# Cross-attention on one core: three weight sums and the eight mask biases made by GpSimd, not VectorE, under a new order table

## The chip, the core and the metric

One core of a Trainium2 chip runs the whole kernel. Its engines are TensorE (PE; its weight loads are shown as PEld), VectorE (DVE), ScalarE (ACT), GpSimd (POOL) and SyncE (SP), which only issues transfers. Each has its own list of instructions and works through it in order; between engines there are semaphores. The metric is the device time of one execution in microseconds (us), lower is better.

## The reference

Eight batches of 256 queries by 1024 features attend to 256 context rows each, with 32 heads of 32 features. All of it is fp32.

```python
mu, var = mean(x), var(x)                       # over the 1024 features
q = ((x - mu) * rsqrt(var + 1e-5) * gamma + beta) @ Wq.T
scores = einsum('bhsd,bhtd->bhst', heads(q), heads(ctx)) / sqrt(32)
probs = softmax(where(mask, scores, -inf))
attn = einsum('bhst,bhtd->bhsd', probs, heads(ctx))
out = x + merge(attn) @ Wout.T
```

Keys and values are both the context itself. The mask has one bit per context row.

## The kernel before, in words

**Slots.** The work is cut into 64 slots, n = 8b + g: batch b, and a group g of four heads (128 features). A slot has, in this order: scores on TensorE (`sc`, 16 matmul records of 256 columns), a softmax on VectorE, ScalarE and GpSimd, and the product of probabilities and values two slots later (`pv`). In the softmax of a slot (`softmax_parts`, from L970) VectorE makes for each head j `e = min(sc + mb, ...)` and its minimum `mn` in one instruction per 128 queries (shown as CUSTOM_DVE_ANT_0 in the profile and as ISA in the order), ScalarE takes the exponential and the sum `den`, VectorE the reciprocal `rden`, GpSimd (for some heads ScalarE) scales `e` by `rden` in two instructions of 256 columns, and VectorE transposes `e` in 32 by 32 blocks into `pT`. `mb` is the mask bias of the batch, 0 or minus 3e38 per context row, made from the mask bytes by `mask_bias` (L919). One buffer serves all batches, so the bias of batch b can be written only when the last `e` of batch b-1 has been made. It is written during slot 8b-2, ahead of the softmax of slot 8b, which stands in the program a slot early.

**Projections.** The query projection (by Wq) of batches 2 to 7 is done for two batches at a time, and the output projection (by Wout) for the two halves of a batch, in Strassen-Winograd form: seven products in place of eight, on sums of blocks of the weights and of the activations. The weight sums T1 to T4 of both matrices are made once, in the first 200 us: `sum_wq` (L840) writes `wq` and, for T1, `ring`; `sum_wo` (L542) writes `wo`. One sum is 128 partitions by 512 elements. T1 = B12 - B11 of Wq has four parts (o = 0 to 3), and T1, T2, T3, T4 of Wout four chunks each (c = 0 to 3), where T4 = B21 - T2. TensorE's products with them are `pq_P` (queries), `po_A` and `po_S` (output). Half of the queries of batches 0 and 1 is made in the same form early on (`ph_P`). `fold` (L725) multiplies gamma into Wq. GpSimd also makes the activation sums (`xnT`, `s`, `at`), adds kept products to the residual (`r<-r,p`), and issues some loads and stores.

**What sets the order.** The kernel is first recorded as a list of calls and then issued in the order of a table of call numbers (`ORDER`, L153; `issue`, L367). So almost every instruction has the line L374 in the profile and is found by its tile names. A second table (`PLAN`, L37) says in which slot each weight sum is recorded and by which engine (`P` GpSimd, `V` VectorE).

```python
def sum_wq(to, o, engine=nc.gpsimd):
    engine.tensor_tensor(weights(to, o), weights(a, o), weights(b, o), ALU.subtract)
...
for n, which, o, *e in WQ_SUMS:
    sums[n].append(partial(sum_wq, which, o, ENGINES[e[0] if e else "P"]))
```

In the table VectorE has three of the 32 weight sums: T1 of Wq, o = 2 and 3 (`ring<-wq`), and chunk 1 of T1 of Wout (`wo<-wo`; the sums of Wout are numbered, 3 is T1).

Of the kernel before, what the change touches and what calls it, by code (L numbers as in the profile page):

```python
# [36 lines left out]
PLAN = {'wq': [[7, 'T1', 0, 'P'], [7, 'T1', 1, 'P'], [10, 'T2', 0, 'P'], [10, 'T2', 1, 'P'], [14, 'T1', 2, 'V'],  # L37
# [116 lines left out]
32-33 35 34 36-38 42 40 43 39 41 50 44 47 52 45-46 54 56 55 58 57 59-60 85 0-15 61-62 64 63 65-66 68 16 69-70  # L154
17 71 18-20 72 21-22 73-77 23-25 80-81 78 83-84 67 86-87 26 79 82 88 27-28 89 29-30 97-98 90-95 101 99 31 102
100 103-112 132 123-126 133 170 96 113 115-117 114 127-130 145-146 171 119-120 131 134 121-122 118 135-136
141-144 147-148 151-156 149-150 157-158 172-173 137 159-160 138-139 163-164 161-162 167 182 165-166 175-177
192-199 290 174 191 348 51 471 49 715 140 168 180 183 178-179 184 169 187-189 185 181 186 190 212 200-201
208-210 202-203 213 211 204 214 205 215 206-207 220-221 216-219 223 222 226-227 230 228-229 231 234 246 252
251 254-256 253 320 318 321 349 48 289 225 224 291 370 236 232-233 244 238 235 247-248 243 237 257-264 273 267  # L160
274 265 275 277 266 278-279 276 268-269 280 498 245 249-250 281-283 285-286 284 271 288 287 53 294-296 311 314
310 313 297 322 332 270 272 333 324-325 472 292-293 500 372 300 298-299 301 326 503 375 302-304 327-331
334-335 376-377 312 315 239 323 340-342 317 352 364 305 343 316 353 381 390-421 336 454 337 455 338-339 382
504-505 356 240 354 344-345 355 360 358 362 306 365 357 359 361 371 307 373 378-380 383-389 456-463 363
422-453 480 464 484 482 486 466 488 490 492 374 465 467 493 481 478 483 476 485 475 487 499 524-525 516-523
526 528 527 529-530 554 347 308 346 241 470 555 469 468 350-351 574 546 501 532 560 506 564 580 242 583
508-509 489 507 510 513 511 533 319 536 531 534-535 512 537 540 538-539 541-542 547 491 576 548-549 558-559
477 544 550 366 561 568 562-563 551 565-567 569 502 577 575 584 515 514 479 657-658 543 585-592 659-664
593-624 673 473-474 625-656 674 683 367 665-666 578-579 689 570 687 667 669 685 693 545 691 695 668 670 684
686 681 678 688 690 677 692 710 717-732 763 700 761 701 494 733-734 694 746 735-736 744 703 756 745 747 771  # L170
775-776 709 741 772 553 552 706 672 705 309 671 770 556-557 778 773 704 869 711 676 675 897 748-749 737
750-755 680 762 495-496 368 708 766 769 767 779 902 908 865 909 696 941 853-854 942 855-860 781-788 863 891
861 764 880 893 738 702 740 739 777 707 774 369 743 742 864 862 886 889 878 882 884 892 881 890 879 883 885
765 866 905 894 937 943 938 944 939-940 789-852 929-936 945 947-949 1000 867-868 912 1572 926 581 712 714 780
716 928 679 713 768 1016 887-888 898-899 910 921-922 895-896 900-901 903 907 906 923 965-968 946 951 950
952-953 969-972 875 911 924 955 757 957-959 954 960-964 977 697-698 984 973-974 571-572 870-871 913 975-976
876 904 914 916 915 497 982-983 873 999 1005 699 573 1017-1019 1224 979 978 986 985 925 682 988-989 980-981
758-759 920 991-993 956 990 995 1015 997 996 1014 1020-1024 1089-1092 1095-1096 872 1025-1088 1105-1106
1097-1098 994 998 1001-1002 1004 1003 919 1113-1116 1109 1107-1108 1110 1118 1111 1120-1121 987 1117 1119 1102
1112 1124 1134 1007 1006 1143 760 1153-1167 1218 1216-1217 917 1145 1011 1360 1122-1123 874 918 1093 1128 1130  # L180
1132 1131 1168 1171-1172 1100 1175-1176 1125-1127 877 1094 1169 1173-1174 1103 1099 1135 1133 1170 1189
1184-1187 1136 1181 1179 1177 1191 1190 1183 1182 1192 1196 1202-1203 1129 1137 1180 1197 1178 1225-1296
1301-1304 1311 1319 1309 1317-1318 1193 1198 1320 1195 1194 1315 1313 1310 1312 1359 927 1101 1149 1199-1200
1104 1013 1204 1209 1138 1210 1215 1147 1144 1140 1208 1305-1308 1150 1333-1335 1330-1331 1201 1316 1325
1327-1328 1151 1142 1323-1324 1321-1322 1340 1188 1337-1338 1326 1339 1152 1220 1346-1347 1205-1207 1146 1141
1009 1139 1008 1214 1212-1213 1010 1148 1219 1314 1348 1362-1369 1373-1378 1297-1298 1379 1299 1380 1300 1387
1385-1386 1329 1336 1381 1342-1343 1345 1383 1388-1389 1344 1349 1390 1382 1384 1401 1391-1393 1398 1396
1405-1406 1332 1397 1399 1410 1415 1407 1414 1412 1411 1420 1437-1444 1357 1370-1372 1509-1512 1640 1361 1394
1402-1403 1395 1221 1358 1222 1404 1408 1517-1518 1350 1341 1352 1211 1351 1525 1527-1528 1416 1519 1526 1409
1538 1413 1400 1417 1419 1355 1418 1428 1531 1540 1536-1537 1529-1530 1532 1539 1567 1570 1430-1431 1541-1542  # L190
1435 1573-1580 1445-1508 1513-1516 1429 1555 1354 1581 1636 1422 1356 1421 1631 1353 1641 1544-1546 1434 1520
1533-1535 1436 1547 1549-1552 1568 1582 1601 1597-1598 1554 1524 1553 1583-1585 1595 1543 1591 1593 1556 1602
1592 1596 1522 1594 1610 1608 1603-1604 1612-1614 1606-1607 1523 1599-1600 1521 1609 1619 1637-1638 1223 1432
1616-1618 1562 1605 1715 1586 1643-1650 1587 1716-1717 1588 1718 1589-1590 1651-1714 1737-1738 1548 1557-1559
1566 1621 1623-1624 1615 1622 1569 1639 1741-1742 1729 1735 1739-1740 1424 1627 1736 1625 1730 1756 1727-1728
1628 1626 1746-1747 1750 1748-1749 1620 1743 1423 1752 1754 1425 1757 1751 1758-1759 1745 582 1744 1764
1782-1789 1719-1720 1776 1721 1777 1722-1726 1778 1790 1807 1805 1761-1763 1806 1809 1642 1803-1804 1753 1799
1765 1791-1795 1810 1733 1808 1824 1426 1801 1767 1820 1563 1816 1818 1814 1839 1560 1629-1630 1561 1760 1766
1427 1633 1611 1632 1826 1825 1802 1768-1770 1731-1732 1800 1817 1815 1832 1564 1838 1012 1772 1844-1853
1796-1797 1854 1798 1855-1857 2050 1780 1433 1821-1822 1827 1565 1571 1773 1933 1811-1813 1734 1774 1858-1920  # L200
1937 1829 1823 1831 1779 1830 1935-1936 1828 1934 1939-1940 1931 1833 1938 1932 1944 1953 1834 1947 1945 1957
1929-1930 1952 1946 1835 1837 1836 1771 1843 1755 1948 1968 1841 1840 1985-1992 1921-1928 1980-1981 2198
1954-1955 1960 1941 1842 1973 1942 1958-1959 1943 1634 2008-2009 2006-2007 1949-1950 1635 1951 1965-1966 1962
1964 1963 1781 1969 1956 1979 1982 1984 1993 2021-2022 1967 1994-1999 2019 2023 2004 2014-2015 2012 1775 1976
1819 2010 2020 2013 2005 1970 2025 2024 2032 2002-2003 1961 1972 1971 2027 2016 2030 2049 2034 2017 2033 2018
1974 2029 2028 2037 2053-2060 2044-2045 2000-2001 2125-2126 2143 2145-2146 2154 2026 2031 2156 2035 2149
2137-2138 2135 2147-2148 2036 2157-2158 2150 2038 2136 2155 2181 2163 2151 2180 2182 2199-2206 2061-2124
2127-2134 2142 2144 2141 2159 2168 2193-2194 2275 2048 2051-2052 1983 2165 2153 2164 2152 2160-2161 2047
2170-2171 2169 2046 2197 2225 2162 2166 2219 2223-2224 2172 2209-2210 2207 2211 2208 2212-2218 2174 2220 2226
2229 2231 2230 2259 2221 2227-2228 2222 2140 2232 2240-2241 2236 2234 2237 2243 2242 2235 2139 2249 2183 2250  # L210
2600 2041 1975 1978 2039 2192 2040 1977 2167 2233 2175 2267 2011 2042 2173 2189 2184 2188 2190 2187 2277-2284
2271 2350-2351 2349 2352-2354 2370-2371 2258 2246 2360-2361 2260 2404-2405 2043 2355-2357 2408 2274 2238 2276
# [126 lines left out]
ALU = mybir.AluOpType  # L339

P = 128
HEADS = 32
LN_EPS = 1e-5
MASKED = 3.0e38
# [35 lines left out]
def xattn_kernel(  # L380
# [11 lines left out]
    nc = tc.nc  # L392
# [43 lines left out]
    nc = Recorded(nc)  # L436
# [113 lines left out]
    mks = {}  # L550
# [1211 lines left out]
```

## Time and profile before

| what | us |
|---|---|
| median of three runs | 564.69 (564.21 to 567.4) |
| the profiled execution itself | 564.37 |
| its span, first to last instruction | 562.6 |
| PE busy | 553.0 |
| DVE busy | 467.3 |
| ACT busy | 436.3 |
| POOL busy | 410.2 |

The times on a page or a timeline are counted from the span's start. A timeline row has start, length, engine, line, operation, output and inputs, how many instructions are merged in it, and in brackets the idle time ahead of it with what ended that. Matmuls in fp32 show two records for one call. A row of the windows view has the busy time of each engine in one stretch and the mean clock that TensorE was granted (1.00 is full). The chain is followed back from the last instruction, at each step to what released it.

### The profile page before, as it was taken

How to read it: one execution, taken by the hardware profiler on the slowest of the kernel's cores; microseconds unless marked ns; L12 is line 12 of the kernel's file. 1: busy time of each engine (PE TensorE's matmuls, PEld its weight loads, DVE VectorE, ACT ScalarE, POOL GpSimd, SP SyncE). 2: the span in 40 equal slices, each digit the busy share in tenths (PEclk: the TensorE clock that was granted, in tenths of full speed). 3: DMA queues.
4: the chain of work that ended last, by engine and by line, in shares of the span. 5: the costliest groups of instructions: out<-in, count | busy, mean ns of one | idle time of the engine just before them, and what ended most of it. 6: DMA issues, size and time to landing. Idle time of an engine off the chain costs nothing.

```text
span 562.6 us, 18616 instructions
## 1 busy us (share of the span) xinstructions
PE 553.0 (98%) x6570; PEld 368.9 (66%) x6570; DVE 467.3 (83%) x1703; ACT 436.3 (78%) x1463; POOL 410.2 (73%) x619
## 2 busy tenths in 40 slices
PE   7999999998999999999999999999999999999997
PEld 6877877655666776667666676666776577645544
DVE  5999999788898889879788889878687888788725
ACT  3698979895896679878877779878869868979920
POOL 2689989897979937569967786477874786367663
PEclk9999999998999999999999999999999999999999
DMA  8988667688558767985767767787766638755433
GB/s 299 378 254 241 179 170 171 182 233 252 144 195 284 258 165 215 246 248 171 202 172 216 210 180 211 231 212 182 222 188 197 201 96 246 205 138 157 119 81 132
DMA packets 48325, 113.67 MB, mean 202 GB/s; under 512 B 9960, under 2 KB 11624, under 8 KB 48232
## 3 DMA queue, kind: packets, MB, share of 16 engines
q1 hardware_dynamic: 42232, 92.55, 58.0%
q0 software_dynamic: 5712, 19.93, 11.5%
q8 instruction: 52, 0.85, 0.6%
q14 instruction: 41, 0.34, 0.2%
q10 hardware_dynamic: 288, 0.01, 0.0%
HBM read 59.91 MB, written 12.70 MB: 129 GB/s over the span
## 4 chain that ended last, share of the span: by engine, by line
PE 90%; DVE 6%; DMA 2%; issue 1%; POOL 1%; ACT 1%; SPq 0%; DVEq 0%; ACTq 0%; POOLq 0%
PE pq_P L374 26%; PE po_S L374 19%; PE sc L374 11%; PE pv L374 11%; PE po_A L374 10%; PE pq L374 4%; PE ph_P L374 3%; PE po_end L374 3%; DVE pT L374 2%; DVE e L374 1%; DMA v_all<-in_kv_dram 1%; PE po_last L374 1%; DVE ring L374 1%; PE px L374 1%; DMA x<-in_x_dram 1%
## 5 line engine op out<-in xcount | busy, mean ns | idle before, releaser
L374 ACT ACTIVATE e<-e,mn 128x256 f32<-128x256 f32 x512 | 256.4, 503 | 60.2 <-DVE mn L374 53.1
L374 POOL TENSOR_SCALAR e<-e,rden 128x256 f32<-128x256 f32 x368 | 172.4, 483 | 105.4 <-DVE rden L374 89.9
L374 DVE STREAM_TRANSPOSE pT<-e 128x512 f32<-128x512 f32 x256 | 175.6, 699 | 31.5 <-POOL e L374 20.2
L374 DVE CUSTOM_DVE_ANT_0 e<-sc,mb 128x256 f32<-128x256 f32 x512 | 191.3, 410 | 6.0 <-PE sc L374 3.8
L374 PE MATMUL pq_P<-xnT,wq 128*128 128x256 f32 x544 | 133.2, 382 | 0.0
L374 PEld LDWEIGHTS pq_P<-xnT,wq 128*128 128x128 f32 x544 | 101.9, 190 | 46.9 <-issue 31.5
L374 ACT ACTIVATION_READ_ACCUMULATOR e<-e,mn 128x1 f32 x512 | 97.4, 190 | 0.0
L374 ACT COPY pc<-pT 128x512 f32<-128x512 f32 x128 | 76.7, 612 | 8.3 <-DVE pT L374 6.0
L374 PE MATMUL po_S<-wo,at 128*128 128x512 f32 x152 | 75.3, 600 | 1.9 <-POOL wo L374 1.9
L374 PE MATMUL po_A<-wo,at 128*128 128x512 f32 x128 | 61.1, 601 | 0.0
L374 PE MATMUL pv<-pT,v_all 64*32 64x128 f32 x3584 | 59.1, 272 | 0.3 <-DMA v_all<-in_kv_dram 0.3
L374 PEld LDWEIGHTS pv<-pT,v_all 64*32 64x32 f32 x3584 | 51.3, 105 | 11.3 <-issue 6.4
L374 DVE RECIPROCAL rden<-den 128x2 f32<-128x2 f32 x228 | 33.1, 152 | 27.8 <-ACT e L374 27.2
L374 PE MATMUL po_S<-wo,s 128*128 128x512 f32 x104 | 51.2, 602 | 0.0
L374 ACT ACTIVATE e<-e,rden 128x256 f32<-128x256 f32 x88 | 41.4, 502 | 11.6 <-DVE rden L374 10.8
L374 PE MATMUL sc<-k,qa 32*128 32x256 f32 x640 | 47.9, 401 | 0.0
L374 DVE DVE_READ_ACCUMULATOR2_ANT mn<- 128x1 f32 x512 | 42.3, 83 | 0.0
L374 ACT COPY at<-pv 128x128 f32<-128x128 f32 x128 | 29.8, 256 | 15.4 <-PE pv L374 15.4
L374 PEld LDWEIGHTS sc<-k,qa 32*128 32x128 f32 x640 | 30.0, 184 | 17.6 <-issue 7.2
L374 PEld LDWEIGHTS po_S<-wo,at 128*128 128x128 f32 x152 | 28.0, 190 | 19.5 <-issue 13.9
L374 PEld LDWEIGHTS po_A<-wo,at 128*128 128x128 f32 x128 | 23.4, 190 | 21.8 <-issue 19.5
L374 PE MATMUL pq_P<-xnT,ring 128*128 128x256 f32 x128 | 33.7, 396 | 0.1
(121 smaller groups left out, 691.3 us busy)
## 6 DMA issues: line engine op xcount, KB each, us to landing
pT<-pT SPq DMA_DIRECT2D x128, 128.0 KB, 3.7
pT<-pc SPq DMA_DIRECT2D x128, 128.0 KB, 3.2
v_all<-in_kv_dram POOLq DMA_DIRECT2D x17, 512.0 KB, 6.0
k<-in_kv_dram SPq DMA_DIRECT2D x30, 256.0 KB, 3.8
r<-in_x_dram SPq DMA_DIRECT2D x26, 256.0 KB, 3.4
xnT<-xe SPq DMA_DIRECT2D x92, 64.0 KB, 3.6
out_dram<-r POOLq DMA_DIRECT2D x18, 256.0 KB, 3.7
wq<-in_wq_dram SPq DMA_DIRECT2D x8, 512.0 KB, 12.2
```

The costliest lines, as they stand in the source:

```text
L374: getattr(getattr(self.nc, other.get(i, engine)), name)(*a, **k)
```

## The change

Four things are edited: three letters in `PLAN`, one line of `mask_bias`, and the order table.

```diff
-        [14, 'T1', 2, 'V'],
-        [14, 'T1', 3, 'V'],
+        [14, 'T1', 2, 'P'],
+        [14, 'T1', 3, 'P'],
...
- 'wo': [[4, 5, 1, 'P'], [4, 5, 0, 'P'], [5, 4, 1, 'P'], [12, 3, 1, 'V'],
+ 'wo': [[4, 5, 1, 'P'], [4, 5, 0, 'P'], [5, 4, 1, 'P'], [12, 3, 1, 'P'],
...
 ORDER = """
-32-33 35 34 36-38 42 40 43 39 41 50 44 47 52 45-46 54 56 55 58 57 59-60 85 0-15 61-62 64 63 65-66 68 16 69-70
+32-33 35 34 37 36 38 42 39 41 40 44 43 56 55 58 57 59-60 85 0-15 61-62 64 63 65-68 16-17 72 18-19 69-71 20-21
...
     def mask_bias(b):
 
         mbs[b] = sm.tile([P, T], F32, tag="mb", name=f"mb_{b}", bufs=1)
-        nc.vector.tensor_scalar(mbs[b], mks.pop(b), 1.0, -MASKED, ALU.subtract, ALU.mult)
+        nc.gpsimd.tensor_scalar(mbs[b], mks.pop(b), 1.0, -MASKED, ALU.subtract, ALU.mult)
```

The calls are the same calls, with the same work for each engine but for these eleven instructions. The order table is new from end to end, so every engine's list is somewhat rearranged. Three places:

**VectorE in slot 14.** `ring<-wq` is the sum for T1 of Wq, `wo<-wo` the one for T1 of Wout. Before:

```order
L374 ISA e_14_2_509,mn_14_2_510<-sc_14_2_497,mb_1_323 128x256
L374 ISA mn_14_2_510 128x1
L374 TENSOR_TENSOR ring_105<-wq_120 128x512
L374 RECIPROCAL rden_14_2_517<-den_14_2_511 128x2
L374 TENSOR_TENSOR wo_126<-wo_126 128x512
L374 RECIPROCAL rden_14_0_512<-den_14_0_505 128x2
L374 STREAM_TRANSPOSE pT_14_501<-e_14_1_506 128x8x64
```

And now, at the end of the same slot's e:

```order
L374 ISA e_14_3_513,mn_14_3_514<-sc_14_3_498,mb_1_323 128x256
L374 ISA mn_14_3_514 128x1
L374 RECIPROCAL rden_14_0_512<-den_14_0_505 128x2
L374 RECIPROCAL rden_14_3_518<-den_14_3_515 128x2
L374 RECIPROCAL rden_14_2_517<-den_14_2_511 128x2
L374 STREAM_TRANSPOSE pT_14_501<-e_14_0_503 128x8x64
```

The two sums are gone from between the last e and the reciprocals of the slot.

**GpSimd in slot 14.** The `wo_126<-wo_126` rows are weight sums of Wout. Before, the first of these two is chunk 2 of T1, the second chunk 3 of T4:

```order
L374 TENSOR_TENSOR xnT_3_384<-xnT_3_384 128x2x256 x2
L374 TENSOR_SCALAR e_14_1_506<-e_14_1_506,rden_14_1_516 128x256 x2
L374 TENSOR_TENSOR wo_126<-wo_126 128x512
L374 TENSOR_SCALAR e_14_0_503<-e_14_0_503,rden_14_0_512 128x256 x2
L374 TENSOR_TENSOR wo_126<-wo_126 128x512
L374 TENSOR_SCALAR e_14_3_513<-e_14_3_513,rden_14_3_518 128x256 x2
```

Now the first is chunk 2 of T4 and the second chunk 3:

```order
L374 TENSOR_TENSOR xnT_3_384<-xnT_3_384 128x2x256
L374 TENSOR_SCALAR e_14_0_503<-e_14_0_503,rden_14_0_512 128x256 x2
L374 TENSOR_TENSOR wo_126<-wo_126 128x512
L374 TENSOR_SCALAR e_14_1_506<-e_14_1_506,rden_14_1_516 128x256 x2
L374 TENSOR_TENSOR xnT_3_384<-xnT_3_384 128x2x256
L374 TENSOR_TENSOR wo_126<-wo_126 128x512
L374 TENSOR_TENSOR wq_120<-wq_120,ring_105 128x512
```

Chunk 3 of T4 still stands near the end of slot 14's scaling. Over GpSimd's whole list, what stands ahead of it now and did not before is the bias of batches 0 and 1, `ring<-wq` for o = 2 and chunk 1 of T1 of Wout; what stood ahead and now follows is one `r<-r,p`.

**The bias of batch 2.** Before, it stood on VectorE between the last e of slot 15, which reads `mb_1`, and the first of slot 16, which reads `mb_2`:

```order
L374 ISA e_15_2_534,mn_15_2_535<-sc_15_2_523,mb_1_323 128x256
L374 ISA mn_15_2_535 128x1
L374 STREAM_TRANSPOSE pT_15_526<-e_15_1_531 128x8x64
L374 TENSOR_SCALAR mb_2_546<-mk_2_412 128x256
L374 RECIPROCAL rden_15_2_542<-den_15_2_536 128x2
L374 BN_STATS st_4_1_519<-x_4_440 128x6
L374 ISA e_16_1_561,mn_16_1_562<-sc_16_1_548,mb_2_546 128x256
```

On GpSimd it now stands here:

```order
L374 TENSOR_SCALAR e_15_1_531<-e_15_1_531,rden_15_1_541 128x256 x2
L374 TENSOR_TENSOR xnT_2_302<-xnT_3_384,xnT_2_302 128x2x256
L374 TENSOR_SCALAR mb_2_546<-mk_2_412 128x256
L374 TENSOR_TENSOR xnT_2_302<-xnT_3_384,xnT_2_302 128x2x256
L374 TENSOR_SCALAR e_15_3_538<-e_15_3_538,rden_15_3_543 128x256
```

It is now between two activation sums on GpSimd. VectorE has two transposes, a variance and a reciprocal between its last read of `mb_1` and its first of `mb_2`. The bias of batch 0 stands on GpSimd behind the issue of a load of `x_2` and one memset.

More of the change, by code (lines that the diff above doesn't have):

```diff
@@ L159 @@
[L159 to L163, printed above, removed]
@@ L209 @@
[L209 to L212, printed above, removed]
-2196 2239 2244 2247-2248 2368 2358-2359 2251 2369 2372 2374-2375 2366-2367 2376 2373 2245 2379 2377-2378
@@ L323 @@
+6462 6459 6461 6545-6546 6463-6494 6496 6495 6497 6458 6499 6457 6449 6498 6566 6507 6552-6553 6547-6548
+6508-6544 6549 6505 6551 6559-6561 6550 6563-6565 6554-6555 6558 6556-6557 6562 6567-6577
 """
```

326 lines of the change are left out of this document (167 added, 159 removed), and 4 rows, old and new, of the table PLAN.

## The prediction

> **What bounds the kernel now.** I read the page first: busy shares, then the chain of waits.
>
> ```profile
> PE 553.0 (98%) x6570; PEld 368.9 (66%) x6570; DVE 467.3 (83%) x1703; ACT 436.3 (78%) x1463; POOL 410.2 (73%) x619
> PE 90%; DVE 6%; DMA 2%; issue 1%; POOL 1%; ACT 1%; SPq 0%; DVEq 0%; ACTq 0%; POOLq 0%
> ```
>
> TensorE is the bound: 90% of the chain that ended last. An edit on VectorE and GpSimd is worth only what TensorE loses to them. So I looked for the stretches in which TensorE loses time: the windows (columns: PE, PEld, DVE, ACT, POOL busy us with instruction counts, granted clock, DMA share, GB/s).
>
> ```profile
> 76.00:84.00 8.00, 7.40 (x159) 5.67 (x144) 7.73 (x36) 7.97 (x26) 5.97 (x13) 1.00 0.59 142
> 84.00:120.00 36.00, 35.67 (x429) 24.38 (x428) 30.18 (x118) 32.17 (x111) 34.13 (x49) 1.00 0.71 187
> ...
> 132.00:139.00 7.00, 4.97 (x11) 2.89 (x11) 6.16 (x24) 4.70 (x18) 5.22 (x8) 0.76 0.93 333
> ...
> 160.00:300.00 140.00, 140.00 (x1768) 94.70 (x1767) 120.09 (x436) 110.96 (x364) 107.34 (x174) 1.00 0.74 213
> ```
>
> From 160 us on TensorE has no gap: 140.00 busy of 140.00, with 20 us idle on VectorE and 33 on GpSimd in the same stretch. Freeing VectorE there gains nothing, and loading GpSimd costs nothing until it is late. Two short windows stand out: 132 to 139, where TensorE is idle 2 us and its clock falls to 0.76, and 76 to 84. The waits view names the first:
>
> ```profile
> PE po_S L374 <- POOL wo L374: 1.9, 1, 1.9
> ```
>
> **What the two stalls cost.** A busy TensorE can still be stretched, so I count what it did against the full rate of the same matmuls, taken from the chain.
>
> ```profile
> 88.04 1.08 PE sc L374 x16
> ...
> 114.07 1.72 PE po_S L374 x4
> ...
> 173.92 2.59 PE pq_P L374 x12
> ```
>
> That is 0.43 us for a 512-wide matmul, 0.216 for a 256-wide one, 1.08 for the 16 of one scores step. Now TensorE's timeline at the first place:
>
> ```profile
> 130.46 1.88 PE L374 MATMUL po_S<-wo,at 128*128 128x512 f32 x4
> 134.22 1.25 PE L374 MATMUL po_S<-wo,at 128*128 128x512 f32 x2 [1.88 <-POOL wo L374]
> 135.62 2.93 PE L374 MATMUL pq_P<-xnT,ring 128*128 128x256 f32 x6
> 138.34 1.11 PE L374 MATMUL po_S<-wo,s 128*128 128x512 f32 x2
> 139.28 0.59 PE L374 MATMUL pq_P<-xnT,ring 128*128 128x256 f32 x2
> ```
>
> Four po_S from 130.46 end at 132.18. Then 2 po_S, 6 pq_P and 2 po_S are 0.86 + 1.30 + 0.86 = 3.02 us, so the last row could stand at 135.20. It stands at 139.28: **4.08 us lost**, 2.04 of them the wait itself (132.18 to 134.22), the rest the low clock behind it and small waits. The second place:
>
> ```profile
> 77.84 2.23 PE L374 MATMUL sc<-k,qa 32*128 32x256 f32 x16
> 80.01 1.56 PE L374 MATMUL ph_P<-xnT,wo 128*128 128x256 f32 x6
> 82.17 1.99 PE L374 MATMUL ph_P<-xnT,wo 128*128 128x256 f32 x8 [0.60 <-DVE qa L374]
> 84.00 1.46 PE L374 MATMUL pq<-xnT,wq 128*128 128x256 f32 x6
> ```
>
> Sixteen scores and 14 matmuls of 256 columns are 1.08 + 3.02 = 4.10 us from 77.84, so the last row could stand at 81.94 and stands at 84.00: **2.06 us lost**.
>
> **Where they come from.** The chain passes, ahead of each, through one very long VectorE instruction, and both are among those that the change removes:
>
> ```profile
> 70.96 3.00 DVE mb L374
> ...
> 125.14 4.99 DVE ring L374
> ```
>
> The timelines of VectorE and GpSimd around the second of them:
>
> ```profile
> 125.06 5.06 DVE L374 TENSOR_TENSOR ring<-wq 128x512 f32<-128x512 f32 x1
> ...
> 130.12 0.66 DVE L374 TENSOR_TENSOR wo<-wo 128x512 f32<-128x512 f32 x1
> ```
>
> ```profile
> 124.94 2.49 POOL L374 TENSOR_TENSOR xnT<-xnT 128x512 f32<-128x512 f32 x2
> ...
> 128.32 1.25 POOL L374 TENSOR_TENSOR wo<-wo 128x512 f32<-128x512 f32 x1
> 132.00 0.94 POOL L374 TENSOR_SCALAR e<-e,rden 128x256 f32<-128x256 f32 x2 [2.43 <-DVE rden L374]
> 132.90 1.27 POOL L374 TENSOR_TENSOR wo<-wo 128x512 f32<-128x512 f32 x1
> ```
>
> The sum of two SBUF operands takes 0.66 us where GpSimd is idle and 5.06 us where GpSimd runs one instruction after another; it ends 0.55 us after GpSimd's last one (129.57). It is kept out for as long as GpSimd has work, 4.40 us. Behind it stood the reciprocals for slot 14: GpSimd sat idle 2.43 us for one, and its next weight sum, the last chunk of T4, ended at 134.17, which is what TensorE waited for. The bias of batch 1 is the same story at 70.9 us:
>
> ```profile
> 70.88 3.08 DVE L374 TENSOR_SCALAR mb<-mk 128x256 f32<-128x256 uint8 x1
> ```
>
> ```profile
> 70.62 1.28 POOL L374 TENSOR_TENSOR ring<-wq 128x512 f32<-128x512 f32 x1
> ...
> 77.64 0.94 POOL L374 TENSOR_SCALAR e<-e,rden 128x256 f32<-128x256 f32 x2 [2.01 <-DVE rden L374]
> ```
>
> The Trainium skill, "SBUF — State Buffer", section "Who interferes with whom", has a rule for this: a VectorE instruction with two SBUF inputs, or in a two-port mode, and a GpSimd instruction share one port pair, and whoever issues first holds it for that whole instruction. The trace agrees that one keeps the other out, but not on the length: the sum waited through five GpSimd instructions (two xnT, two e, one wo), not one. By the rule alone its wait would be at most about 1.28 us, and the place would give back some 1.2 us, not 4; I go by the row.
>
> **The change, part by part.** Prices on GpSimd come from the groups by shape; the row of the bias on VectorE (ns: min/median/max) gives its low end.
>
> ```profile
> L374 POOL TENSOR_SCALAR e<-e,rden 128x256 f32<-128x256 f32 x368 | 172.4, 483 | 105.4 <-DVE rden L374 89.9 <-PE sc L374 6.3 <-ACT pc L374 4.1
> ...
> L374 POOL TENSOR_TENSOR wo<-wo 128x512 f32<-128x512 f32 x15 | 19.1, 1277 | 0.0
> ```
>
> ```profile
> L374 DVE TENSOR_SCALAR mb<-mk x8: 265/342/3080, 12.3 to 473.9; 128x256 f32<-128x256 uint8 x8
> ```
>
> *Removed from VectorE:* three sums and eight biases. Their ordinary part (0.66 and 0.34 us each) lies under a gap-free TensorE and is worth nothing; the two blocked ones are worth the 4.08 and 2.06 us. No other VectorE instruction between 30 and 540 us reads two SBUF tensors, so nothing takes their place at that port.
>
> *Added to GpSimd:* three sums at 1.28 us (same shape as the wo row) and eight biases. A bias from uint8 is not in the trace on GpSimd: between 0.27 (the least on VectorE) and 1.28 (a sum of twice the width); I take 0.48, the row of its width. In all 3 x 1.28 + 8 x 0.48 = 7.7 us. The third sum and six biases fall where GpSimd is busy 107 of 140 us: 0. What counts is the stretch up to 134 us, where it is nearly full (34.13 of 36 us): there the last T4 sum now has two sums and the bias of batch 1 more ahead of it (batch 0's lies where GpSimd waits at the start), 2 x 1.28 + 0.48 = 3.04, and the new order has put one r add of 1.27 behind it: net 1.77. Given back are the two idle times, 2.43 and 2.01. So it would end at 134.17 - 4.44 + 1.77 = 131.50. TensorE, 2.06 us earlier, asks for it at 132.18 - 2.06 = 130.12. The wait that is late next is thus 0 to 1.4 us; I take 0.7. T1's sum for Wout caused no wait when it ended at 130.78, and now stands ahead of slot 13's scaling.
>
> *Added waits:* a bias was in order on VectorE by itself. Now GpSimd must wait until VectorE has read the old bias for the last time, and VectorE's first e of the next batch waits for GpSimd. Behind it on VectorE stand the rest of that softmax, and behind that TensorE's values. Seven hand-overs; at most a sum and the bias lie in between (1.28 + 0.48 = 1.76 us, the place of batch 2), at least nothing, since a transpose or two of 0.7 us stand between the two reads. VectorE's 20 idle us in 140 cover that; I take 0.4 for all. If the cover were gone it would be 7 x 1.76 = 12.3.
>
> *At the start:*
>
> ```profile
> 12.97 0.72 POOL L374 DMA_DIRECT2D x<-in_x_dram  x1 [3.75 <-DMA wq<-in_wq_dram]
> ```
>
> ```profile
> 13.66 0.41 DVE L374 CUSTOM_DVE_ANT_0 e<-sc,mb 128x256 f32<-128x256 f32 x1
> ```
>
> Batch 0's bias now follows that DMA issue and a memset on GpSimd: 12.97 + 0.72 + some 0.5 + 0.48 = 14.7, so the first e comes 1 us later. TensorE has the rest of the first projections to do meanwhile: 0 to 1 us, taken as 0.3.
>
> *The new order table* elsewhere keeps the same instructions; TensorE without a gap leaves nothing to gain, and a loss would be a stall like the one above, 2 to 4 us. I take 0 and keep this for the range.
>
> Sum, against the profiled execution's own 564.37 us (span 562.6 and 1.8 around it; the median of the runs, 564.69, lies 0.3 above): 564.37 - 4.08 - 2.06 + 0.7 + 0.4 + 0.3 = **559.6 us**. A measurement of this kernel can tell about 0.5% (2.8 us) from no change.
>
> **The rivals.**
>
> *GpSimd stays the late one.* It is nearly full before 134 us, and the change adds to it there. If the wait for T4 comes back at its old size, only 2.06 us are gained: 562.3. If in addition none of the 4.44 idle us return, T4 ends at 135.94, 5.8 us after TensorE asks; with the 2.04 behind the wait that is 7.9 against 6.14 lost now: 566.1. Against it: both idle times waited for a reciprocal, behind the instructions that go. 0.22.
>
> *The hand-overs decide (slower).* Price 12.3 if none is covered: 564.37 - 6.14 + 12.3 = 570.5. It is slower than before from the point where half of it (6.1) reaches TensorE. For it: the VectorE-to-GpSimd waits are GpSimd's largest (89.9 us by the row above), so it is often a step behind. Against it: TensorE hides all of those from 160 us on. 0.10.
>
> *The clock does not come back.* The row shows 0.76 in the one window with a long wait, and 1.00 in the others. If the low clock is not due to that wait, its 2.0 us stay: 561.7. The Trainium skill, "TensorE: Matmul & The Clock Gate", Part 1, lets the clock fall only after an idle window of about 3.4 us; by that rule a wait of 1.88 us would not do it. 0.05.
>
> **How the numbers follow.** Forecast as worked out: 0.63, own range 557.6 (no added term costs anything and the table wins a little) to 561.6. The clock rival also lies over 0.5% below. So faster 0.68, within 0.5% 0.22, slower 0.10. The range reaches from 557.6 over the first rival's end, 566.1; it leaves out the hand-overs and the least likely gains.
>
> **What would show it.** Right: no VectorE instruction over 1.5 us between 60 and 150 us; a granted clock of 1.00 from 76 to 160; TensorE's wait for wo under 1.4 us; GpSimd busy 7 to 8 us longer; 0.48 us a bias. Wrong: a longer wait for wo or for a projection's T1 than before; VectorE idle on GpSimd's mb by more than 1 us at a batch's start with TensorE waiting for pT behind it; a gap on TensorE after 160 us.

## The result, and the profile after

The changed kernel is **slower**: median 567.49 us of 21 runs (564.75 to 571.82) beside 563.43 us of before on the same chip (560.59 to 567.4), ratio 1.0074, 95% interval 1.0055 to 1.0094. The forecast was 559.6. All ratios leave out runs more than 1.5% above the fastest of their kernel, so they are not the quotients of the medians. The profiled execution is the slowest of the 21, 571.82 us with a span of 569.7. The page after, busy times and the chain by engine:

```profile
PE 557.1 (98%) x6570; PEld 372.4 (65%) x6570; DVE 458.1 (80%) x1692; ACT 436.7 (77%) x1463; POOL 422.3 (74%) x630
PE 77%; POOL 6%; SPq 5%; DMA 4%; ACT 4%; DVE 2%; issue 1%; DVEq 0%; POOLq 0%; ACTq 0%
```

VectorE lost 9.2 us of work, GpSimd took on 12.1 (forecast: 7.7). TensorE's share of the chain fell from 90% to 77%, and SyncE with the DMA now hold 9% of it. The windows after, with one more at 340 us:

```profile
76.00:84.00 8.00, 8.00 (x178) 6.17 (x176) 6.80 (x29) 6.96 (x22) 7.83 (x10) 1.00 0.63 161
84.00:120.00 36.00, 34.68 (x418) 23.90 (x415) 29.89 (x114) 30.61 (x102) 35.08 (x50) 1.00 0.69 185
132.00:139.00 7.00, 6.67 (x143) 4.58 (x141) 5.41 (x18) 4.41 (x12) 6.39 (x9) 1.00 0.82 211
160.00:300.00 140.00, 140.00 (x1726) 94.25 (x1732) 118.65 (x431) 108.71 (x359) 110.28 (x175) 1.00 0.77 216
340.00:352.00 12.00, 9.63 (x41) 6.20 (x40) 7.15 (x27) 9.76 (x29) 8.30 (x12) 0.86 0.77 218
```

Both places of the forecast did what it said: 76 to 84 and 132 to 139 are nearly full, at a clock of 1.00. But 84 to 120 is not full any more, and at 340 us there is a new hole with a low clock. TensorE's waits:

```profile
PE sc L374 <- DMA k<-in_kv_dram: 2.4, 1, 2.4
...
PE pq L374 <- DVE xnT L374: 0.9, 1, 0.9
PE pq L374 <- DVE qa L374: 0.9, 1, 0.9
```

**The wait at 345 us.** TensorE's timeline, then SyncE's, of the changed kernel; then SyncE's of before:

```profile
343.78 1.46 PE L374 MATMUL pq_P<-xnT,ring 128*128 128x256 f32 x6
347.61 2.09 PE L374 MATMUL sc<-k,qlo 32*128 32x256 f32 x16 [2.37 <-DMA k<-in_kv_dram]
349.63 1.80 PE L374 MATMUL pq_P<-xnT,ring 128*128 128x256 f32 x4
```

```profile
340.88 0.43 SPq L374 DMA_DIRECT2D k<-in_kv_dram  x1
```

```profile
321.56 1.26 SPq L374 DMA_DIRECT2D k<-in_kv_dram  x1
```

The same load, the context of slot 40, was issued at 321.56 us before, 21.5 us ahead of its first use. The new table issues it at 340.88, 4.4 us before TensorE asks, and it lands 6.6 us later. Behind the wait TensorE runs at half rate (four 256-wide matmuls in 1.80 us, 0.43 each where 0.216 is full).

**The start.** GpSimd, VectorE and TensorE after:

```profile
15.79 0.73 POOL L374 DMA_DIRECT2D x<-in_x_dram  x1 [6.40 <-PE px L374]
16.52 0.49 POOL L374 MEMSET qlo<- 128x448 f32 x1
17.11 1.09 POOL L374 TENSOR_SCALAR mb<-mk 128x256 f32<-128x256 uint8 x1
```

```profile
18.23 0.42 DVE L374 CUSTOM_DVE_ANT_0 e<-sc,mb 128x256 f32<-128x256 f32 x1 [1.68 <-POOL mb L374]
```

```profile
19.39 1.58 PE L374 MATMUL pq<-xnT,wq 128*128 128x129 f32 x8 [0.88 <-DVE xnT L374]
```

Batch 0's bias stands where the forecast put it, behind a load's issue and a memset. But that issue, which waits for TensorE's px, came 2.8 us later than before (15.79 beside 12.97; why: the second group below), the bias took 1.09 us, and the first e comes at 18.23 (before 13.66, forecast 14.7). An xnT stands behind it on VectorE, and TensorE waits 0.88 us for that.

**Where TensorE lost time.** The starts of its matmuls against the full rate of those before them, as in the prediction's working, summed by stretch (us):

| profile | 0-20 | 20-40 | 60-100 | 100-120 | 120-140 | 140-340 | 340-360 | 380-420 | all |
|---|---|---|---|---|---|---|---|---|---|
| before | 4.4 | 1.5 | 3.6 | 1.2 | 4.4 | 5.6 | 0.5 | 1.4 | 29.5 |
| after | 8.5 | 2.4 | 3.1 | 1.6 | 1.5 | 6.4 | 4.4 | 1.2 | 37.0 |
| before_long_burst | 4.3 | 1.5 | 3.6 | 0.8 | 1.3 | 6.0 | 0.5 | 1.1 | 25.9 |
| sums_only_old_table | 6.0 | 1.3 | 3.6 | 0.7 | 2.5 | 6.0 | 0.6 | 1.3 | 29.0 |
| table_only | 5.1 | 2.2 | 3.9 | 2.1 | 0.8 | 7.3 | 3.9 | 1.2 | 34.1 |
| biases_back | 7.3 | 2.1 | 4.2 | 1.9 | 0.6 | 7.2 | 0.5 | 1.4 | 32.8 |
| bias0_back | 6.4 | 1.9 | 2.7 | 2.0 | 0.7 | 6.4 | 0.6 | 5.9 | 34.3 |

Stretches left out (40 to 60, 360 to 380, from 420 on) are in the last column. Two of the later columns jump from profile to profile (340 to 360, 380 to 420), and so do the first and 120 to 140: a single profile tells only one throw of these.

### The profile page after: what moved, and what is told of

Same layout as the page of the kernel before. It is cut to its first block, busy times and chain, and to the rows that moved or that the text cites. A ratio compares the mean times of both kernels' runs of the same rounds, so it can differ in the third digit from the quotient of the medians.

```text
span 569.7 us, 18622 instructions
## 1 busy us (share of the span) xinstructions
PE 557.1 (98%) x6570; PEld 372.4 (65%) x6570; DVE 458.1 (80%) x1692; ACT 436.7 (77%) x1463; POOL 422.3 (74%) x630
## 4 chain that ended last, share of the span: by engine, by line
PE 77%; POOL 6%; SPq 5%; DMA 4%; ACT 4%; DVE 2%; issue 1%; DVEq 0%; POOLq 0%; ACTq 0%
PE pq_P L374 23%; PE po_S L374 17%; PE sc L374 10%; PE pv L374 10%; PE po_A L374 9%; SPq L374 5%; PE po_end L374 3%; POOL e L374 2%; PE ph_P L374 2%; ACT e L374 2%; PE po_last L374 1%; POOL wq L374 1%; DMA k<-in_kv_dram 1%; PE pq L374 1%; DMA pT<-pc 1%
## 5 line engine op out<-in xcount | busy, mean ns | idle before, releaser
L374 ACT COPY at<-pv 128x128 f32<-128x128 f32 x128 | 29.8, 253 | 14.8 <-PE pv L374 14.7
L374 PEld LDWEIGHTS po_S<-wo,at 128*128 128x128 f32 x152 | 28.1, 190 | 18.1 <-issue 14.7
L374 PE MATMUL pq<-xnT,wq 128*128 128x256 f32 (+3 forms) x144 | 32.7, 368 | 1.8 <-DVE xnT L374 0.9
```

The lines of the kernel that those rows point to most:

```text
L374: getattr(getattr(self.nc, other.get(i, engine)), name)(*a, **k)
```

## The experiments

Ratios are to runs of before on the same chip, with 95% intervals. From the two profiles I held **theory 1**: a late start (4.1 us), one late load (3.9), less the stalls won. **Theory 2**: the biases cost the time. **Theory 3**: the new table does.

### Table or engines

*table_only*: before, with the new table.

```diff
-32-33 35 34 36-38 42 40 43 39 41 50 44 47 52
+32-33 35 34 37 36 38 42 39 41 40 44 43 56 55
...
```

> The new order table, with the three sums and the eight biases left on VectorE. Base: medians 563.43 before and 567.49 after. Theory 1 (three places): the engine move won the two old stalls (6.1 us in the profiled run), and the loss is a late first softmax (4.1 us, batch 0's bias on GpSimd behind a load that waits for TensorE) and one context load issued too late by the new table (2.4 us of wait at 345 us, 3.9 us with the low clock behind it). By it the start is back near 13.7 us for the first e, the wait at 345 us stays, and the time is 563.4 + 3.9 + about 1 for other small waits = 568 (566 to 570). Theory 2 (the bias on GpSimd costs the time, the table nothing): 563.4, at most 1.5 off. Theory 3 (the table costs it all, the engine move pays what was forecast): 567.5 + 3.8 = 571.

Measured: 1.0093 (1.0056 to 1.0130), median 570.57. The table alone has a worse ratio than the whole change, though the intervals overlap. Theory 2 (563.4) falls; 1.0093 of 563.43 is 568.7, in theory 1's range. The first e came at 14.20 us. The same k load, issued at 338.48 us, was late here too (3.9 us lost in 340 to 360). The waits view puts that wait of 1.7 us down to a reciprocal on VectorE, but the first weight load behind it starts at 344.79, before that reciprocal ends (344.80) and just after the wait for the k load does (344.77).

*engines_only*: the changed kernel with the old table.

```diff
-32-33 35 34 37 36 38 42 39 41 40 44 43 56 55
+32-33 35 34 36-38 42 40 43 39 41 50 44 47 52
...
```

> The old order table, with the three sums and the eight biases on GpSimd. In the old table batch 0's bias stands ahead of the third x load on GpSimd, and the context load of slot 40 early on SyncE. Theory 1 (three places): no late first softmax, no wait at 345 us, the two VectorE stalls gone: 563.4 - 6.1 + 1 to 2 for the fuller GpSimd before 134 us = 558 to 560. Theory 2 (the bias on GpSimd, 1.08 us each and seven hand-overs): 567.5, as after. Theory 3 (the table alone): 563.4 - 3.8 = 559.6, the forecast.

Measured: **1.0233** (1.0197 to 1.0269), 577.08: all three theories missed. One place explains most of it. GpSimd, then TensorE:

```profile
69.58 1.07 POOL L374 TENSOR_SCALAR mb<-mk 128x256 f32<-128x256 uint8 x1 [8.84 <-DVE mn L374]
```

```profile
78.85 1.56 PE L374 MATMUL ph_P<-xnT,wo 128*128 128x256 f32 x6
89.89 2.50 PE L374 MATMUL ph_P<-xnT,wo 128*128 128x256 f32 x5 [9.47 <-DVE qa L374]
```

In the old table batch 1's bias stands where VectorE, in order by itself, has already read the old one. In GpSimd's list that place is early: GpSimd stands 8.84 us until VectorE has read the old bias for the last time, and everything queued behind it is late, up to TensorE. It is the mechanism of the prediction's second rival. That the price given there, 12.3 us, is near the measured 12.7 is luck: it stood for seven waits of at most 1.76 us each, and this is one of 8.84. A second bias buffer was not tried.

*biases_back*: the changed kernel with the biases on VectorE.

```diff
-        nc.gpsimd.tensor_scalar(mbs[b], mks.pop(b), 1.0, -MASKED, ALU.subtract, ALU.mult)
+        nc.vector.tensor_scalar(mbs[b], mks.pop(b), 1.0, -MASKED, ALU.subtract, ALU.mult)
```

> The changed kernel with the eight biases on VectorE again; the three sums stay on GpSimd. Theory 1: the first softmax is on time (4.1 us back), the stall at 76 to 84 us may come back (up to 2.1), the wait at 345 us stays: 567.5 - 4.1 + 0 to 2.1 = 563.4 to 565.5. Theory 2 (the bias on GpSimd costs the time): 563.4 - 4.1 (the gain of the sums alone) = 559.3, up to 561. Theory 3 (the table): 567.5 or 2 more.

Measured: 1.0028 (1.0004 to 1.0051), median 566.21. 1.0028 of 563.43 is 565.0, in theory 1's range, but not for theory 1's reasons: in this profile the first e comes at 16.74 us, and nothing is lost at 345 us. Against after (1.0074), the eight biases on GpSimd cost 0.46%, 2.6 us.

*context_load_early*: the changed kernel, one load moved.

```diff
-3812 3601 3671 3670 ... 3602 3877 3803
+3812 3601 3877 3671 3670 ... 3602 3803
```

> The changed kernel with one call moved in the table: the context load of slot 40, issued at 340.9 us, stands on SyncE three other loads' worth earlier (behind the r load of 327.5 us). Theory 1: no wait of TensorE for k near 345 us, full clock from 340 to 360 us, the first e still at 18.2 us: 567.5 - 2.4 to 3.9 = 563.6 to 565.1 if the wait comes in most executions; nothing if it came in the profiled one alone. Theory 2: 567.5. Theory 3: between 563.6 and 567.5, since other places of the table stay.

Measured: 1.0081 (1.0052 to 1.0110). In its profile the wait at 345 us is gone (0.7 lost in 340 to 360), in the median nothing is won. Of the six profiles that keep the new table's place for this load, three lose about 4 us there (after, after_long_burst, table_only) and three do not, so theory 1 loses its second term as the main explanation of the median; an average gain of up to about 1.6 us would not show within these two intervals.

With *sums_only_old_table* (next group) this gives a table of ratios:

| | all on VectorE | sums on GpSimd | all eleven on GpSimd |
|---|---|---|---|
| old table | 1 | 1.0033 (1.0005 to 1.0062) | 1.0233 (1.0197 to 1.0269) |
| new table | 1.0093 (1.0056 to 1.0130) | 1.0028 (1.0004 to 1.0051) | 1.0074 (1.0055 to 1.0094) |

Under the new table the sums' move wins 0.65% and the biases' loses 0.46%, with intervals that don't touch. Under the old one the biases lose 2.0%, and the sums win nothing. The new table costs 0.93% by itself and saves 1.6% of what all eleven cost without it.

### The start's clock, and the stall at 132 us

The same px matmuls in before and in after:

```profile
8.39 0.49 PE L374 MATMUL px<-ring,x 128*128 128x128 f32 x3
```

```profile
8.37 0.85 PE L374 MATMUL px<-ring,x 128*128 128x128 f32 x3
```

Start to start it is 0.109 us a matmul before and 0.213 after, until 13.1 us. The profile's granted clock says 1.00 in both; in after, the first change of the clock that the trace holds is the rise at 13.10 us, so the column says nothing about the time ahead of it. The first 16 `busy` matmuls, made to warm TensorE up, take 3.41 us at half rate in every profile, and only what follows differs. The Trainium skill, "TensorE: Matmul & The Clock Gate", Part 1, has a window of about 3.4 us that runs free of the kernel and lets the clock up once it has been busy. The trace agrees: with the same matmuls, full rate begins at 7.0 us or before in table_only, at 10.5 in context_load_early, at 12.8 in biases_back, and in all 20 profiles the changes of the granted clock lie whole multiples of 3.413 us apart.

*before_long_burst* and *after_long_burst* make the burst longer, to 24 and 26 matmuls, and shorten the pause ahead of the first px (after_long_burst with 22-31):

```diff
-85 0-15 61-62
+85 0-15 24-31 61-62
```

> The kernel before, with the 16 warm-up matmuls at the start made 24: eight of the later fillers are moved into the first burst, so that TensorE pauses under 0.2 us instead of 1.6 us before its first px. Theory 1 (start clock): TensorE's first chain runs at full rate (0.109 us a 128-wide matmul) in some executions and at half rate (0.213 us) in others, as the burst happens to fall; half rate costs 2.7 to 3 us. If the kernel before has that chance as well, its median falls by 1 to 2 us, to 562 to 563 beside 563.4 to 564.4. If it starts at full rate nearly always: within 0.7 us of before. Theory 2 (the start does not matter to the difference): the same, within 0.7.

> The changed kernel, with the 16 warm-up matmuls made 26 in the same way, up to the first px at 7.0 us (the pause was 2.0 us). Theory 1 (start clock): three of four profiles with the new table ran their first chain at half rate, 7.0 to 10.4 or 13.0 us, so most executions gain 2.7 to 3 us: 567.5 - 2 to 3 = 564.5 to 565.5, and px at 0.109 us each in the profile. Theory 2 (the loss lies behind the start, in the table's order of the softmax and in the biases on GpSimd): 567.5, at most 1 us less.

Measured: 0.9981 (0.9950 to 1.0013) and 1.0065 (1.0030 to 1.0101). In all six profiles with a long burst px runs at full rate at once; with the burst of 16 in five of 14 (before, one_sum_moved, engines_only, table_only, three_transfers_early), with either table. In a sixth, bias0_back, it begins at full rate and falls to half from 8.2 to 11.6 us (granted clock 0.50). So the half rate is a chance that both kernels have, worth 1.6 us in the first 20 (6.0 beside 4.4 under the old table). It made the profile of after look worse than its median, and is not the difference between the two.

before_long_burst shows a second chance. VectorE and GpSimd at the place of the 5.06 us sum:

```profile
124.47 0.69 DVE L374 TENSOR_TENSOR ring<-wq 128x512 f32<-128x512 f32 x1
```

```profile
124.74 2.77 POOL L374 TENSOR_TENSOR xnT<-xnT 128x512 f32<-128x512 f32 x2 [0.44 <-DMA xnT<-xe]
```

Table and engines are those of before from 20 us on. GpSimd had paused 0.44 us for a transfer, the sum got in first and took 0.69 us. In the profile of before GpSimd's xnT began at 124.94, 0.12 us ahead of the sum, which took 5.06. So which of the two got in first was a race, lost there by 0.12 us. It is lost often: of the five profiles in which VectorE makes this sum under the old table, it took 5.06, 5.05 (old_then_new), 5.11 (burst_and_t4_first) and 2.84 us (t4_sum_first), and 0.69 only here. Here the window has no gap, and 120 to 140 loses 1.3 us in place of 4.4:

```profile
132.00:139.00 7.00, 7.00 (x36) 4.00 (x35) 6.18 (x23) 6.49 (x25) 6.18 (x9) 1.00 0.92 318
```

*table_burst_load*: table_only with the long burst and the early load.

```diff
-85 0-15 61-62 ... 3601 3671 ... 3602 3877 3803
+85 0-15 22-31 61-62 ... 3601 3877 3671 ... 3602 3803
```

> The new table with the engines of before, the long burst, and the context load of slot 40 moved earlier. The table alone was 1.0093 of before (569.6 beside 564.35). Theory 1: the table's loss is the start at half rate (2.7 to 3 us) and the late context load (2.4 us of wait and 1.1 to 1.5 behind it): 569.6 - 6 = 563 to 564, no slower than before. Theory 2 (many small waits spread over the table): 567 to 569.

Measured: 1.0034 (0.9994 to 1.0075), from 1.0093, between the two theories. The difference is only just clear of the two intervals together: the start and the load are part of the table's cost, and whether they are all of it this run does not show.

*sums_only_old_table*: the old table, the three sums alone moved.

```diff
-        [14, 'T1', 2, 'V'],
-        [14, 'T1', 3, 'V'],
+        [14, 'T1', 2, 'P'],
+        [14, 'T1', 3, 'P'],
...
- [12, 3, 1, 'V'],
+ [12, 3, 1, 'P'],
```

> The old table with the three sums on GpSimd and the eight biases left on VectorE: only the first part of the change, without a new table. With all eleven moved it was 1.0233 of before, and 9.5 us of that was one wait of TensorE behind the bias of batch 1. Theory A (the forecast's first term holds without a new table): the wait at 132 us goes, 563.9 - 4.08 + 0.7 = 560.5. Theory B (the table must move with the engines): the three sums stand ahead of the last T4 sum in GpSimd's list and TensorE waits for it about as long as before (the kernel with all eleven moved waited 1.8 us for wo): 563 to 565. Under both, no GpSimd instruction waits 8.8 us for VectorE near 70 us.

Measured: 1.0033 (1.0005 to 1.0062). Theory B holds. With no sum on VectorE TensorE still waits for T4:

```profile
135.21 1.12 PE L374 MATMUL po_S<-wo,at 128*128 128x512 f32 x2 [1.78 <-POOL wo L374]
```

and in table_only, with all three sums on VectorE, 120 to 140 loses 0.8:

```profile
132.00:139.00 7.00, 7.00 (x35) 4.42 (x37) 6.93 (x26) 5.32 (x19) 7.00 (x9) 1.00 0.82 194
```

What removed that stall in the changed kernel is thus the new table; the order of GpSimd's sums in it is the likely part, which *t4_sum_first* below tries alone.

### One instruction at a time

*one_sum_moved* and *burst_and_one_sum*: before, with only the long sum on GpSimd; the second with the long burst too.

```diff
-OTHER = {}
+OTHER = {1641: 'gpsimd'}
```

> The kernel before with one instruction moved: the sum that took 5.06 us on VectorE (T1 of Wq, o = 2) is made by GpSimd, at its place in the old table; the two other sums and the biases stay. Theory P (the stall of 4.08 us at 132 us is in every execution and hangs on this sum): 564.0 - 4.1 + 0.5 = 560.5. Theory R (a race: the sum is shut out only when GpSimd starts its next instruction 0.1 us ahead of it, as in the first profile, and not when GpSimd has just paused, as in the profile with the longer burst, where the same sum took 0.69 us): the stall is in part of the executions, so the median falls by 1 to 2.5 us, to 561.5 to 563. Theory Q (GpSimd's own 1.28 us for it makes the last T4 chunk late again, as with all three sums moved): 564 to 565, with a wait for wo of over 1 us.

> The kernel before with the longer burst (24 warm-up matmuls; alone 0.9981 of before, 561.9) and the one long VectorE sum on GpSimd. Theory P: 561.9 - 3.6 = 558.3. Theory R: 560 to 561.5, and fewer executions above 564 than with the burst alone, since both chances (the start's clock and the shut-out sum) are taken away. Theory Q: 562 to 563.

Measured: 1.0002 (0.9979 to 1.0025) and 1.0005 (0.9977 to 1.0032). Theory P falls: the instruction on which the forecast hung 4.08 us is worth nothing that can be measured. TensorE waits 1.0 and 1.1 us for wo in the two profiles, so Q's own 1.28 us on GpSimd is there. The first of them:

```profile
PE po_S L374 <- POOL wo L374: 1.0, 1, 1.0
```

A gain of up to 0.2%, 1.2 us, would still lie within the interval.

*engines_only_bias1_back*: engines_only, with the bias of batch 1 on VectorE.

```diff
-OTHER = {}
+OTHER = {779: 'vector'}
```

> The old table with everything on GpSimd but the bias of batch 1, which goes back to VectorE. With it on GpSimd the kernel was 1.0233 of before (577), GpSimd waited 8.84 us ahead of that bias for VectorE's last read of the old one, and TensorE 9.47 us behind it. Theory 1 (one place: the instruction stands too early in GpSimd's list, and all behind it waits): 577.3 - 9.5 - about 1.5 of low clock = 566, near the old table with the sums alone moved (1.0033, 566). Theory 2 (all seven hand-overs cost): over 571.

Measured: 1.0077 (1.0047 to 1.0107), from 1.0233: one instruction's place cost 1.6%, 8.8 us. Theory 1 is shown for the old table.

*bias0_back*: the changed kernel, batch 0's bias on VectorE.

```diff
-OTHER = {}
+OTHER = {96: 'vector'}
```

> The changed kernel with only the bias of batch 0 back on VectorE. With all eight back it was 1.0028 of before against 1.0074, so the eight cost 2.6 us. Theory 1 (the start: batch 0's bias stands on GpSimd behind the issue of the third x load, which waits for TensorE, and a memset, and TensorE then waits about 1 us for a xnT behind the first e): 1 to 1.7 us back, 1.0045 to 1.0055, 566.5 to 567. Theory 2 (the seven later hand-overs): 1.007 to 1.008, as after. Theory 3 (the start is all of it): 1.003.

Measured: 1.0051 (1.0022 to 1.0080), where theory 1 has it; the interval also reaches 1.0074, so the size stays rough: about half of the biases' 0.46%. Two profiles that start at full rate agree: the first 20 us lose 6.4 in three_transfers_early, with this bias on GpSimd (first e at 15.60 us), and 5.1 in table_only, with it on VectorE (14.20). The profile of bias0_back shows a third place that comes and goes (5.9 us lost in 380 to 420, before 1.4). GpSimd and TensorE:

```profile
398.27 1.27 POOL L374 TENSOR_TENSOR xnT<-xnT 128x512 f32<-128x512 f32 x1 [5.30 <-DMA ring<-kept_T]
```

```profile
PE sc L374 <- DVE mn L374: 2.5, 1, 2.5
```

The scaling of e stands behind that xnT in GpSimd's list. One piece of the xe copy that it reads was issued at 360 us before and at 390 to 396 under the new table, beside 512 KB loads. The waits view names a kept_T load issued 0.6 us ahead of that piece; GpSimd's sequencer held for that piece's own semaphore until 398.18.

### Mending the table

*three_transfers_early* and *all_mended* (the second also with bias 0 on VectorE and the long burst):

```diff
-698 870 ... 573 497 920 ... 3601 3671 ... 3602 3877 3803 ... 4222 4418 ... 4489 4284 4490
+497 698 870 ... 573 920 ... 3601 3877 3671 ... 3602 3803 ... 4222 4284 4418 ... 4489 4490
```

> The changed kernel with three transfers earlier in the table, where SyncE issues them: the context load of slot 40 (lead over its first use 6.7 us in the changed kernel, 21.5 before), one piece of the transposing copy of xe for the last batch pair (5.7 us, 30 before), and the factors of slot 4 (3 to 7 us). Of seven profiles with the new table three show TensorE waiting 1.9 to 2.5 us at 343 us for the first, three 1.3 to 2.6 us at 397 to 403 us behind the second, and all of them 0.5 to 1.7 us at 100 us behind the third. Theory T (short leads in the new table's transfers): the waits at 343 and 397 go in every execution, the one at 100 us shrinks, the median falls by 2 to 4 us from 1.0074 to 1.001 to 1.004, and the slowest executions by more (after had 571.8, this under 569). Theory U (the loss is spread, the transfers are a few unlucky executions): 1.006 to 1.008.

> The changed kernel with the three transfers early, the bias of batch 0 on VectorE, and the long burst at the start. Theory T with the start: 1.0074 less 0.0035 to 0.006 (transfers), 0.002 (bias 0) and 0 to 0.003 (burst): 0.997 to 1.002 of before, 562 to 565. Theory U: 1.004 or more.

Measured: 1.0049 (1.0020 to 1.0078) and 1.0029 (0.9997 to 1.0062), between theories T and U. In all_mended, 384 to 400 us, GpSimd hardly waits for xe any more, but ScalarE waits for another copy, as it had for 3.0 us in bias0_back:

```profile
ACT pc L374 <- DMA pT<-pc: 3.9, 1, 3.9
...
POOL xnT L374 <- DMA xnT<-xe: 0.6, 1, 0.6
```

TensorE waits 1.8 and 1.1 us there. One transfer moved is thus not enough there. How full the DMA engines are does not explain it: their share from 390 to 400 us is 0.84 in this profile and 0.94 in biases_back, where TensorE has no gap.

*t4_sum_first* and *burst_and_t4_first*: before, two GpSimd sums changing places; the second with the long burst.

```diff
-1435 1573-1580 ... 1533-1535 1436 1547
+1436 1573-1580 ... 1533-1535 1435 1547
```

> The kernel before with two weight sums on GpSimd changing places: the last chunk of T4 goes where chunk 2 of T1 stood (it ended at 129.57 in the first profile, and TensorE asks for T4 at 132.18), and T1's chunk to T4's place (it is used 8 us later). Nothing moves between engines. Six profiles with the old table show TensorE waiting 0.7 to 2.1 us near 132 us whichever engine made the sums, and those with the new table none. Theory O (that wait is a matter of the order of two sums): no wait for wo near 132 us, and 1.3 to 3.9 us less where it was: 0.995 to 0.998 of before. Theory E (a matter of the engine of the long sum): 1.000, the wait stays in part of the executions.

> The kernel before with those two sums changing places and the long burst at the start; all engines as before. The burst alone was 0.9981 of before, with a profile of 560.8. Theory O: 0.993 to 0.996 of before, 560 to 562, and the best of all kernels here. Theory E: 0.998, like the burst alone.

Measured: 1.0018 (0.9987 to 1.0049) and 0.9991 (0.9959 to 1.0023). No wait for wo is left in either profile, as theory O said, but no time is won. In the second the long sum took 5.11 us on VectorE, and TensorE waits at the same place for a qa instead:

```profile
PE pq_P L374 <- ACT qa L374: 2.4, 1, 2.4
```

*new_then_old* and *old_then_new* split the table at about 200 us: each takes one table's order up to one matmul (call 2342) and the other's for the rest; the first has the engines of after and is shown against it, the second those of before.

```diff
-2338-2342 2343-2348 2362 2382-2384 2276
+2338-2342 2275 2189 2188 2260 2404 2276 2382-2383
...
```

> The changed kernel, all eleven instructions on GpSimd, with the new table for what it places up to about 200 us and the old table's order for the rest. Theory T (the late part of the new table costs through transfers with short leads at 343 us and 390 to 403 us, each in about half of the executions, 1.9 us a run on average each): 1.0074 less 0.005 to 0.007 = 1.0005 to 1.0025 of before, 563.5 to 565, and a narrower spread than the changed kernel's 564.8 to 571.8. Theory V (the loss lies in the early part, start, biases and the waits up to 105 us): 1.006 to 1.008.

> The kernel before, all eleven instructions on VectorE, with the old table up to about 200 us and the new table's order for the rest. Theory T: all of the late waits, none of the early ones: 1.004 to 1.007, 565.5 to 567.5, with the slowest executions over 569. Theory V: 0.999 to 1.002.

Measured: 1.0111 (1.0080 to 1.0142) and 1.0044 (1.0014 to 1.0074). The new late half does cost something with the engines of before, as theory T has it. But the old late half does not mend the changed kernel, so T is not the whole. The seam is not clean: the first has new waits of 1.1 us for a reciprocal at 211 us and of 0.6 us near 483 us, there for a GpSimd sum that has a bias in its old place 2 us ahead of it.

No version here beats before beyond its interval; the long burst alone, 0.9981, is the nearest.

## Why the prediction was wrong, step by step

The forecast's terms, beside what the table of ratios gives for each (in us, of 563.4; each measured one is uncertain by about 2):

| term | forecast | measured |
|---|---|---|
| the new order table | 0 | +5.2 |
| three sums, under the new table | -3.4 (4.08 won, 0.7 lost) | -3.7 |
| eight biases, under the new table | -1.4 (2.06 won, 0.4 and 0.3 lost) | +2.6 |

The sums' agreement is luck: the stall at 132 us, on which that term was built, is not there in table_only, and what moving them won under the new table was not found.

**The new order table, "I take 0": the step that failed.** It cost 0.93% alone, 5.2 us, in at least three kinds: transfers issued shortly before they are needed (345 us, 390 to 403 us, each in some of the executions), small waits near 30, 85 and 100 to 105 us (table_only loses 8.2 us in 20 to 40 and 60 to 120, before 6.3), and 0.7 us at the start. Another 1.7 us, between 140 and 340 us, was not traced. A TensorE without gaps was read as "nothing to gain", but it also says that nothing pays for a loss. The lead of each transfer was in the trace of before and in the two orders, and was not worked out.

**"Worth 4.08."** It was priced from one execution. The long sum was shut out in four of five such profiles; the one in which it was not, with the long burst, lost 3.1 us less there with the same engines and table. And the engine alone did not set T4's end: with the long sum moved TensorE still waited 1.0 to 1.1 us, with all three 1.8; under the new table it waited for none, whoever made the sums. The reading of the 5.06 us instruction was right, the step from it to the end of T4 was only argued. The 0.7 us for a wait that comes late next did not appear under the new table.

**"Worth 2.06."** 76 to 84 us did become full. This stall was no chance: the bias of batch 1 took 3.05 to 3.11 us in every old-table profile that has it on VectorE. But 60 to 100 loses 3.1 where it lost 3.6, as the next wait takes more than half of the rest:

```profile
88.22 1.56 PE L374 MATMUL pq<-xnT,wq 128*128 128x256 f32 x6 [0.86 <-DVE qa L374]
```

What would be late next was worked out for T4, not here.

**The price of a bias.** 0.48 us was taken, 1.08 measured, within the bounds:

```profile
L374 POOL TENSOR_SCALAR mb<-mk 128x256 f32<-128x256 uint8 x8 | 8.6, 1080 | 1.0 <-DVE mn L374 0.4
```

The row of its width has fp32 at both ends, this one reads bytes. Alone that is 4.8 us more on GpSimd, mostly hidden.

**The hand-overs (0.4 taken) and the second rival.** In the changed kernel GpSimd waits 0.4 us in all for the last read, and VectorE 1.8 us for the seven later biases. So the rival's mechanism is not what made it slower; the new table prevents it. Without that table it is there, at 1.6%. The prediction had the mechanism, spread over seven small waits where one large one came, and did not see that the table is what decides it.

**The start (0.3 taken, bounds 0 to 1).** Bias 0 costs about 0.23% (1.3 us, the interval is wide), over the upper bound; of what looked like 4.1 us in the profile, about half is the chance of the clock.

**The clock, third rival.** It came back: 1.00 in 132 to 139. The rule that the prediction cites there from the Trainium skill, "TensorE: Matmul & The Clock Gate", Part 1 (the clock falls only after an idle window of about 3.4 us), is not borne out as a length of one pause: in after it fell behind a wait of 2.4 us. The rival's 561.7 is 0.48% below 564.37, not over 0.5%.

**The signs.** Three signs of being right came: in after, no VectorE instruction between 60 and 150 us is longer than 1.25 us, the granted clock is 1.00 from 76 to 160, and TensorE does not wait for wo. Two did not (12.1 us more on GpSimd, 1.08 us a bias). These signs covered the stalls that the change aimed at. The sign of being wrong that came is the gap on TensorE after 160 us, and it came from the table.

What stays open: how the table's 0.93% divides over its early and late half, as the two split kernels do not add up; where the half of the biases' 2.6 us that is not bias 0 is lost; and how often each of the waits that come and go is there.

## What to carry to other kernels

Price a stall by several executions: what hangs on which of two instructions starts 0.1 us earlier is a chance, and so is part of its gain. When an order table is replaced, work out for every transfer its lead over the first use, in the old and in the new order, and ask of each instruction that changes its engine what stands behind it there while it waits. Where the busiest engine has no gap, a new order has nothing to win there, and can lose.

## What the runs showed of the hardware that was not expected

- TensorE's rate after a warm-up burst of 16 matmuls, 3.41 us, is a chance: full at once and for good in 5 of 14 profiles, and in all six with a burst of 24 or 26. The granted-clock column shows 1.00 ahead of the first change on record, while matmuls start 0.213 us apart in place of 0.109.
- A single wait of about 2 us can halve TensorE's rate (before, 135.1 to 138.5 us, after a wait of 1.88; after, 347.6 to 351.0, after 2.37). In the traces all rises and falls of the granted clock within a profile are whole multiples of 3.413 us apart, and a fall lasts one such stretch (three in engines_only, behind the wait of 9.47). Between 20 and 550 us of the 20 profiles, half rate followed on each of these stretches in which TensorE was idle for 1.88 us or more, and on none with 1.66 or less; of the two in between, 1.69 (table_only) was followed by it and 1.78 (sums_only_old_table) was not. So what falls into one stretch seems to count, more than the length of a wait: the wait of 1.83 us in all_mended lay across two, and the clock stayed at 1.00.
- On GpSimd a 128x256 instruction that reads bytes and writes fp32 takes 1.08 us, the same with fp32 at both ends 0.48.
- A VectorE sum of two SBUF tensors took 0.69 or 5.06 us with the same engines and table from 20 us on, as it came 0.27 us ahead of GpSimd's next instruction or 0.12 us behind it.
